# Four graph layers on one core: the start of layer 1 written as one list of 58 steps

## The chip, the cores and the metric

The kernel runs on one core of a Trainium2 chip. Its time is the device time of one execution in microseconds (us). A core has five engines that run side by side, each with its own queue of instructions that it works off in order: TensorE (PE, with PEld for the loading of weights), VectorE (DVE), ScalarE (ACT), GpSimd (POOL) and SyncE (SP, which here only issues transfers). They wait for one another through semaphores, and a waiting instruction holds up everything behind it in its own queue.

## The reference, cut to what matters

There are 2708 nodes with 128 features, and a sparse adjacency matrix of 2708 x 2708 with some 16 entries in a row. Four layers follow one another, each `x = x + layer(relu(layernorm(x)), adj)`. The change is at the seam of layers 0 and 1:

```python
# layer 0: columns of adj, weighted sum over the degree
h = jnp.maximum(_layernorm(x, axis=-1), 0.0)
msg = jnp.matmul(adj.T, h)
inv_deg = 1.0 / adj.sum(axis=0)            # 0 where it is infinite
x = x + msg * inv_deg[:, None]
# layer 1: a message for every pair of nodes, summed with the weights of adj
h = jnp.maximum(_layernorm(x, axis=-1), 0.0)
s = h @ msg_w[:, :D].T                     # source part
d = h @ msg_w[:, D:].T                     # destination part
messages = gelu(s[:, None, :] + d[None, :, :] + msg_b)
aggregated = jnp.einsum('ijd,ij->id', messages, adj)
new = jnp.concatenate([h, aggregated], axis=-1) @ upd_w.T + upd_b
g = gelu(new) + h
x = x + layernorm(g) * ln_w + ln_b
```

Layers 2 (a GRU cell) and 3 (two attention heads over the neighbours) aren't touched.

## The kernel before, in words

**Tiles.** The 2708 rows are cut into 22 tiles of 128 (`NT`), and these into six groups of four tiles, the last of two (`GROUPS`). The columns are cut into 22 blocks of 124 (`NB`, `JB`).

**Layer 0** reads `adj` tile by tile. PE multiplies it with the normed rows into six banks, and turns it around for a copy `adjT` in memory that layers 2 and 3 use. DVE scans it: for every row and every block the eight largest values (`val`) and their columns (`col`), by one `max` and one `max_index` each, 484 of each. This list of entries is what layer 1 works from. The sums of layer 0 lie turned (features down, nodes along) in `sumT`, whose memory is also `hT`, the turned input of layer 1.

**Layer 1** treats the listed entries alone. For a tile `t` it builds, step by step:

- `count_rows(t)`: how many entries each row has in each block (`rows_n`).
- `rank(t)`: a product with the triangle `before` gives, for each block, how many entries stand ahead of a row's own (`ends`, `ends4`).
- `select_rows(t)`: a compare gives the 0/1 matrix `sel` (entry slot against row), and two transfers bring a copy of it moved by one row, `later`. `finish_rows(t)` subtracts the copy, which leaves one row per slot.
- `describe(t)`: packs values (split into three bfloat16 parts), columns and `ends` into `xb`. There are two such buffers.
- `fetch(t, half)`: 11 small products of `sel` and `xb` bring each slot its row's description. `place(t)` picks from it the slot's own value and column (`value`, `where`) and builds `mine`.
- `pass_on(t)`: `where` is turned on PE, copied on ACT (`where_T`), written to memory and read back to all partitions (`spread`). `columns(t)` compares it into `cols`.
- `put_values(t)` (8 blocks on POOL) and `put_more(t, k)` (14 blocks on ACT, in five shares) make `put`, which carries a slot's value into its row.

Then the main work: `combine(t, k)` takes four blocks at a time, six products each (three for the source part with `sel` and `s3`, three for the destination part with `cols` and `d3`), `activate(t, k)` takes Gelu of them on ACT, and `gather(t, k)` sums them with `put`. `sources(k)` makes `s3` for two tiles, and the term of the diagonal. `s3` and `d3` are numbers split into three bfloat16 parts: a cast on ACT, a subtract on DVE into a scratch tile, a cast on ACT, and a subtract on POOL (the helper `split`).

**Periods.** `period(t)` lays the steps of several tiles side by side: the main work of tile `t`, `put`, `pass_on` and `columns` of `t+1`, `fetch` and `place` of `t+2`, and `rank`, `describe`, `select_rows` and `finish_rows` of `t+3`. The whole of layer 1 stands in `tc.manual_schedule()`: each engine's queue has its instructions in the order in which the program text makes them.

**The prologue** brings in what the first period needs. For each group `g` it has four steps. `enter(g)` turns the sums back on PE, adds them to `xs` on DVE (scaled by `inv_deg`), and takes the statistics of the norm, with a power on POOL (`moments`, L116 to L119). `rows_and_turn(g)` has five small DVE operations (`factors`, L125 to L129) and the norm with Relu on ACT (`scale_rows`, L135). `turn_rows(g)` turns these rows into `hT` on PE with a copy on ACT (L153, L155). `destinations(g)` multiplies them with `msg_w` into `p_d` and splits that into `d3` (L324 to L327). The groups run as a pipeline of depth four, and whole periods are put between them: `period(-3)` after the round of group 0, `period(-2)` after that of group 2, `period(-1)` after that of group 4. `sources(0)` comes at the end, then `period(0)`.

Three buffers matter in what follows: `p_m` (two banks, for `enter` and for `combine`), the tag `r` (one bank, for `p_r` of `rank`, `p_w` of `pass_on`, `p_s` of `sources` and `p_u`), and the tag `sb` (one scratch tile, for `sources` and for the split of `destinations`).

The constants of layer 1 (`count`, `count_h`, `ident_h`, `part`, `before`, the zeroed `later`, the row numbers in `xb`) lie in a pool that is opened after layer 0 and takes over its memory.

Of the kernel before, what the change touches and what calls it, by code (L numbers as in the profile page):

```python
# [20 lines left out]
F32 = mybir.dt.float32  # L21
# [9 lines left out]
P = 128  # L31
# [24 lines left out]
def width(b):  # L56
    return min(JB, N - b * JB)
# [3 lines left out]
def listed_layers(ctx: ExitStack, tc: tile.TileContext, x, adj, w, out, flag):  # L61
# [8 lines left out]
    def bank(name):  # L70
        return ps.tile([P, CH], F32, tag="ps", name=name)
# [73 lines left out]
    def span(t, k):  # L145

        return t * P, min(k * P, N - t * P)
# [18 lines left out]
    total = keep.tile([P, NT], F32, name="total")  # L166
    inv = keep.tile([P, NT], F32, name="inv_deg")

    sumT = keep.tile([D, N], F32, name="hT1")
# [102 lines left out]

    HB = NB // 2
    HP = 8
    R = 4
    C = 4 * S + R + 1  # L280
    with (
        tc.tile_pool(name="l1c", bufs=1) as fix,
        tc.tile_pool(name="l1i", bufs=2) as work,
# [18 lines left out]
        count = fix.tile([P, P], F32, name="count")  # L302
        nc.gpsimd.iota(count, [[1, P]], base=0, channel_multiplier=0, allow_small_or_imprecise_dtypes=True)
        count_h = fix.tile([P, P], BF16, name="count_h")
        nc.vector.tensor_copy(count_h, count)
        ident_h = fix.tile([P, P], BF16, name="ident_h")
        nc.vector.tensor_copy(ident_h, ident)
        part = fix.tile([P, 1], F32, name="part")
        nc.gpsimd.iota(part, [[0, 1]], base=0, channel_multiplier=1, allow_small_or_imprecise_dtypes=True)
        before = fix.tile([P, P], BF16, name="before")  # L310
        nc.vector.tensor_scalar(before, count, part, None, ALU.is_gt)
        ends4 = fix.tile([P, NB, R], BF16, name="ends4")
        rows_n = fix.tile([P, NT, NB], BF16, name="rows_n")
        ends = fix.tile([P, NT, NB], BF16, name="ends")
        later = fix.tile([P, NB, E], BF16, name="later")
        nc.gpsimd.memset(later, 0.0)
        d3 = fix.tile([P, NB, 3, D], BF16, name="d3")
        xb = [fix.tile([P, NB, C], BF16, name=f"xb{q}") for q in range(2)]
        for q in range(2):
            nc.vector.tensor_copy(xb[q][:, :, 4 * S : 4 * S + R], part.unsqueeze(1).to_broadcast([P, NB, R]))  # L320

        def split(dst, src, rest):

            nc.scalar.copy(dst[0], src)  # L324
# [268 lines left out]

        GB = (NB + 3) // 4

        def period(t):

            now, c, b, a = (0 <= t + q < NT for q in range(4))
            last = 0 <= t - 1 < NT
            if c:  # L600
                put_values(t + 1)
            for k in range(GB):
                if now:
                    combine(t, k)
# [24 lines left out]
                if k > 0 and c:  # L629
                    put_more(t + 1, k)  # L630
                if k == 3 and c:
                    columns(t + 1)
                if k == 3 and b:
                    place(t + 2)
                if k == 4 and a:
                    finish_rows(t + 3)


        def enter(g):

            t, k = GROUPS[g]
            p = mpool.tile([P, 4, D], F32, name="p_m")
            for q in range(k):
                m = size(t + q)
                nc.tensor.transpose(p[0:m, q, :], sumT[:, (t + q) * P : (t + q) * P + m], ident)
            for q in range(k):
                m = size(t + q)
                nc.vector.scalar_tensor_tensor(
                    xs[0:m, t + q, :], p[0:m, q, :], inv[0:m, t + q : t + q + 1], xs[0:m, t + q, :],
                    op0=ALU.mult, op1=ALU.add,  # L650
                )
            state["m", g] = moments(tiles_of(xs, t, k), "n1")

        def rows_and_turn(g):
            t, k = GROUPS[g]
            scale_rows(tiles_of(h, t, k), tiles_of(xs, t, k), *factors(*state.pop(("m", g))), AF.Relu)

# [5 lines left out]
        done = [0]  # L663

        def destinations(g):

            c, n = span(*GROUPS[g])
            while done[0] < NB and done[0] * JB + width(done[0]) <= c + n:
                b0 = done[0]
                bn = 1  # L670
                while bn < 4 and b0 + bn < NB and (b0 + bn) * JB + width(b0 + bn) <= c + n:
                    bn += 1
                p = bank("p_d")
                pv = p.rearrange("p (b d) -> p b d", b=4)
                for b in range(b0, b0 + bn):
                    k = width(b)
                    nc.tensor.matmul(pv[0:k, b - b0, :], hT[:, b * JB : b * JB + k], msg_wT[:, 1, :], start=True, stop=True)
                rest = once.tile([P, 4, D], F32, tag="sb", name="d_r")
                whole = bn if width(b0 + bn - 1) == JB else bn - 1
                for q0, q1, k in ((0, whole, JB), (whole, bn, width(NB - 1))):  # L680
                    if q1 > q0:
                        split(
                            [d3[0:k, b0 + q0 : b0 + q1, q, :] for q in range(3)], pv[0:k, q0:q1, :], rest[0:k, q0:q1, :]
                        )
                done[0] = b0 + bn
# [837 lines left out]
```

## Time and profile before

| | |
|---|---|
| time, median of three | 1119.21 us (1118.8 to 1120.24) |
| span of the profiled execution | 1117.6 us |
| PE busy | 966.6 us, 86% of the span |
| DVE busy | 840.2 us, 75% |
| ACT busy | 504.0 us, 45% |
| POOL busy | 393.4 us, 35% |
| end of the scan (last `max_index`, DVE) | 241.7 us |
| first product of `combine(0, 0)` | 313.66 us |
| first Gelu of `activate(0, 0)` | 317.85 us |

The upper rows are averages over stages that have different limits, and say little on one of them. The lower three, from the timeline, mark out the stage that is changed: from the end of the scan to the first Gelu. The 40 slices of the span show it as a dip of PE (a digit is the busy share in tenths):

```profile
PE   3988887932489999999999988999979999999993
DVE  5999999997647667687777364656668987997673
```

One slice is 27.9 us. DVE is at 9 up to the ninth slice (layer 0), PE falls to 3, 2 and 4 in slices 9 to 11, and stands at 9 from the twelfth on, through the periods of layer 1.

### The profile page before, as it was taken

The page shows a single profiled execution, that of the slowest core. Times are in us where ns is not written, and L with a number is a line of the kernel's source. Part 1 is how long each engine was busy: PE and PEld are TensorE (multiplying, and loading weights), DVE is VectorE, ACT ScalarE, POOL GpSimd, SP SyncE. Part 2 cuts the span into 40 slices and gives each one's busy share as a digit, 9 for nine tenths or more (in the row PEclk, how much of TensorE's full clock was granted, in tenths as well). Part 3 has the DMA queues.
Part 4 walks back from the last instruction along what each step waited for, and adds up shares of the span by engine and source line. Part 5 has one row for each costly group of instructions (what it writes and reads, how often), then busy time and mean ns, then how long its engine had stood idle before and what let it go on. Part 6 is the DMA issues. An engine that isn't in the chain of part 4 may idle for free. (4 is left out here: it accounts for less than half of the span.)

```text
span 1117.6 us, 21914 instructions
## 1 busy us (share of the span) xinstructions
PE 966.6 (86%) x7968; PEld 763.3 (68%) x7968; DVE 840.2 (75%) x2948; ACT 504.0 (45%) x1319; POOL 393.4 (35%) x466
## 2 busy tenths in 40 slices
PE   3988887932489999999999988999979999999993
PEld 1554444512379999989898953444468899999772
DVE  5999999997647667687777364656668987997673
ACT  3966656622556666666665631433322200230143
POOL 3111112102546656666665343354301200250132
PEclk9999898755589999999999988999989999999996
DMA  9497886521113332232332046555300000000000
GB/s 357 187 312 261 309 294 241 186 61 51 53 56 102 106 105 102 82 106 79 105 105 79 28 144 211 186 198 199 99 18 1 1 9 1 1 20 1 2 15 14
DMA packets 55298, 125.39 MB, mean 112 GB/s; under 512 B 7414, under 2 KB 19782, under 8 KB 52472
## 3 DMA queue, kind: packets, MB, share of 16 engines
q1 hardware_dynamic: 48590, 121.12, 31.2%
q10 hardware_dynamic: 6590, 2.77, 1.0%
q8 instruction: 64, 1.05, 0.4%
q14 instruction: 54, 0.44, 0.1%
HBM read 77.30 MB, written 30.84 MB: 97 GB/s over the span
## 5 line engine op out<-in xcount | busy, mean ns | idle before, releaser
L804 PE MATMUL att<-hv,wt 128*128 128x129 f32 (+2 forms) x1936 | 240.7, 281 | 9.2 <-DVE wt L772 9.2
L804 PEld LDWEIGHTS att<-hv,wt 128*128 128x128 f32 (+2 forms) x1936 | 221.8, 190 | 26.3 <-DVE wt L772 8.7
L772 DVE SCALAR_TENSOR_TENSOR wt<-row,lift,mask 128x1024 f32<-128x1024 f32 (+5 forms) x176 | 160.0, 939 | 34.2 <-PE att L804 34.1
L423 POOL TENSOR_SCALAR put<-mine,value 128x128 f32<-128x128 bf16 x176 | 144.8, 839 | 74.2 <-DVE mine L339 71.8
L499 PE MATMUL p_m<-s,sel 128*128 128x128 bf16 x1452 | 161.9, 220 | 7.7 <-ACT g L511 4.7
L503 PE MATMUL p_m<-d,cols 124*128 124x128 bf16 (+1 forms) x1452 | 161.7, 219 | 1.4 <-DVE cols L453 1.3
L119 POOL TENSOR_TENSOR n_r<-n_r,minus_half 128x4 f32<-128x4 f32 (+1 forms) x36 | 48.3, 1343 | 298.5 <-DVE n_r L118 289.6
L196 PE MATMUL acc<-a,hs 128*128 128x512 f32 (+2 forms) x264 | 122.3, 599 | 24.7 <-DMA a<-in_adj 17.9
L524 PE MATMUL agg<-put,g 128*128 128x128 f32 (+1 forms) x968 | 135.9, 281 | 0.0
L925 PE MATMUL p_agg<-a,hs 128*128 128x512 f32 (+2 forms) x264 | 111.1, 562 | 8.2 <-DVE u L572 4.1
L524 PEld LDWEIGHTS agg<-put,g 128*128 128x128 f32 x968 | 118.2, 192 | 0.0
L217 DVE FIND_INDEX8 col<-val,a 128x8 uint16<-128x124 f32 (+1 forms) x441 | 117.9, 278 | 0.0
L499 PEld LDWEIGHTS <-sel 128*128 128x128 bf16 x1452 | 104.1, 98 | 13.3 <-issue 9.5
L503 PEld LDWEIGHTS <-cols 124*128 124x128 bf16 (+1 forms) x1452 | 102.3, 98 | 2.5 <-DVE cols L453 1.9
L511 ACT ACTIVATE g<-p_m 128x512 f32<-128x512 f32 x132 | 73.0, 553 | 65.6 <-PE p_m L503 64.5
L216 DVE MAX8 val<-a 128x8 f32<-128x124 f32 (+1 forms) x441 | 101.8, 269 | 0.0
L431 ACT ACTIVATE put<-mine,value 128x128 f32<-128x128 bf16 x308 | 100.5, 390 | 0.0
L225 PEld LDWEIGHTS p_T<-ident,a 128*128 128x128 f32 x484 | 59.6, 147 | 56.3 <-ACT aT L229 27.0
L196 PEld LDWEIGHTS acc<-a,hs 128*128 128x128 f32 (+1 forms) x264 | 49.4, 207 | 69.0 <-issue 41.8
L225 PE MATMUL p_T<-ident,a 128*128 128x128 f32 x484 | 78.4, 295 | 20.8 <-DMA a<-in_adj 10.2
L229 ACT ACTIVATE aT<-p_T 128x512 f32<-128x512 f32 (+2 forms) x132 | 70.9, 540 | 43.6 <-issue 16.8
L925 PEld LDWEIGHTS p_agg<-a,hs 128*128 128x128 f32 (+1 forms) x264 | 48.5, 196 | 57.0 <-issue 56.0
(228 smaller groups left out, 1407.1 us busy)
## 6 DMA issues: line engine op xcount, KB each, us to landing
a<-in_adj SPq DMA_DIRECT2D x21, 1354.0 KB
adjT<-aT SPq DMA_DIRECT2D x105, 256.0 KB
a<-adjT SPq DMA_DIRECT2D x20, 1280.0 KB
spread<-passed SPq DMA_DIRECT2D x22, 704.0 KB
later<-sel SPq DMA_DIRECT2D x22, 616.0 KB
later<-sel SPq DMA_DIRECT2D x22, 82.5 KB
adjT<-aT SPq DMA_DIRECT2D x21, 74.0 KB
a<-adjT SPq DMA_DIRECT2D x4, 370.0 KB
```

The lines of the kernel that those rows point to most:

```text
L196: nc.tensor.matmul(accs[ci][:, 0:cw], h[0:m, n, :], a[0:m, c : c + cw], start=(n == 0), stop=(n == NT - 1))
L216: nc.vector.max(val[:, n, b, :], ab)
L217: nc.vector.max_index(col[:, n, b, :], val[:, n, b, :], ab)
L225: nc.tensor.transpose(p[0:k, q * P : q * P + m], a4[0:m, q, j * P : j * P + k], ident[0:m, 0:m])
L423: nc.gpsimd.tensor_scalar(st["put", 0][:, b, :], st["mine"][:, b, :], st["value"][:, b : b + 1], None, ALU.mult)
L431: nc.scalar.activation(st["put", 1][:, b - HP, :], st["mine"][:, b, :], AF.Identity, scale=st["value"][:, b : b + 1])
L499: nc.tensor.matmul(p[:, b - b0, :], st["sel"][:, b, :], s3[:, q, t % 2, :], start=(q == 0), stop=False)
L503: nc.tensor.matmul(p[:, b - b0, :], st["cols"][0:kb, b, :], d3[0:kb, b, q, :], start=False, stop=(q == 2))
L524: nc.tensor.matmul(agg, g[:, b - 4 * k, :], put, start=(b == 0), stop=False)
L772: nc.vector.scalar_tensor_tensor(wt[0:kj, :], row[0:kj, k, c : c + n], lift[0:kj, j, k : k + 1], mask[0:kj, j, c : c + n], op0=ALU.max, op ...
L804: nc.tensor.matmul(banks[s // 3][0:m, s % 3, :], wt[0:kj, q * P : q * P + m], hv[0:kj, j, k, :], start=(v < 2 and s // 3 not in touched), ...
L925: nc.tensor.matmul(pa[:, 0:n], h[0:k, j, :], a[0:k, j - j0, 0:n], start=(j == 0), stop=(j == NT - 1))
```

## The change

It does three things. The constants of layer 1 are made ahead of layer 0, in a pool that stays open through both layers. The pipeline over groups with whole periods between is replaced by one list of 58 small steps in an order written by hand, in which `enter`, `rows_and_turn` and `destinations` are each cut in two (`spread_sums` and `enter`; `rows` and `turn_rows`; `destinations` up to the first cast, and `split_destinations`). And the last two groups' destinations are put into period 0 (`fourth` ahead of `combine(0, 0)`, `fifth` ahead of `combine(0, 1)`), where the puts of tile 1 move behind them. A part of `destinations` now always takes four blocks, `4 * g` onwards, where it took as many as the turned rows allowed. The arithmetic is the same. The aim is to keep the engines from standing still one after the other between the two layers.

```diff
@@ ahead of layer 0
+    count = keep.tile([P, P], F32, name="count")
+    nc.gpsimd.iota(count, [[1, P]], base=0, ...)
+    count_h = keep.tile([P, P], BF16, name="count_h")
+    nc.vector.tensor_copy(count_h, count)
+    ident_h = keep.tile([P, P], BF16, name="ident_h")
+    nc.vector.tensor_copy(ident_h, ident)
+    part = keep.tile([P, 1], F32, name="part")
+    nc.gpsimd.iota(part, [[0, 1]], base=0, ...)
+    before = keep.tile([P, P], BF16, name="before")
+    nc.vector.tensor_scalar(before, count, part, None, ALU.is_gt)
...
+    later = keep.tile([P, NB, E], BF16, name="later")
+    nc.gpsimd.memset(later, 0.0)
+    xb = [keep.tile([P, NB, C], BF16, name=f"xb{q}") for q in range(2)]
+    for q in range(2):
+        nc.vector.tensor_copy(xb[q][:, :, 4 * S : 4 * S + R], part.unsqueeze(1).to_broadcast([P, NB, R]))
@@ after layer 0: the same lines, with fix.tile for keep.tile, are taken out
@@ def period
-        def period(t):
+        def period(t, between=()):
...
-            if c:
+            if c and not between:
                 put_values(t + 1)
             for k in range(GB):
+                for step in between[k : k + 1]:
+                    step()
                 if now:
                     combine(t, k)
@@ enter, rows, destinations
-        def enter(g):
+        def spread_sums(g):
 
             t, k = GROUPS[g]
             p = mpool.tile([P, 4, D], F32, name="p_m")
             for q in range(k):
                 m = size(t + q)
                 nc.tensor.transpose(p[0:m, q, :], sumT[:, (t + q) * P : (t + q) * P + m], ident)
+            state["p", g] = p
+
+        def enter(g):
+
+            t, k = GROUPS[g]
+            p = state.pop(("p", g))
...
-        def rows_and_turn(g):
+        def rows(g):
...
+        def blocks_of(g):
+
+            return 4 * g, min(4, NB - 4 * g)
 
         def destinations(g):
 
...
+            for src, dst, q0, q1, k in state["d", g]:
+                nc.scalar.copy(dst[0], src)
+
+        def split_destinations(g):
+
+            rest = once.tile([P, 4, D], F32, tag="sb", name="d_r")
+            for src, dst, q0, q1, k in state.pop(("d", g)):
+                r = rest[0:k, q0:q1, :]
+                nc.vector.tensor_tensor(r, src, dst[0], ALU.subtract)
+                nc.scalar.copy(dst[1], r)
+                nc.gpsimd.tensor_tensor(dst[2], r, dst[1], ALU.subtract)
@@ the order
         with tc.manual_schedule():
-            for t in range(4):
-                count_rows(t)
-            steps = (enter, rows_and_turn, turn_rows, destinations)
-            fill = {0: -3, 2: -2, 4: -1}
-            for g in range(len(GROUPS) + len(steps) - 1):
-                for k in reversed(range(len(steps))):
-                    if 0 <= g - k < len(GROUPS):
-                        steps[k](g - k)
-                if g in fill:
-                    period(fill[g])
-            sources(0)
-            for t in range(NT + 1):
+            for step, n in (
+                (spread_sums, 0), (count_rows, 0), (spread_sums, 1), (rank, 0), (enter, 0),
+                (select_rows, 0), (describe, 0), (enter, 1), (spread_sums, 2), (rows, 0), (turn_rows, 0),
+                (count_rows, 1), (rows, 1), (count_rows, 2), (count_rows, 3), (destinations, 0), (turn_rows, 1),
+                (finish_rows, 0), (fetch_both, 0), (rank, 1), (enter, 2), (spread_sums, 3), (select_rows, 1),
+                (split_destinations, 0), (destinations, 1), (describe, 1), (rows, 2), (turn_rows, 2),
+                (place, 0), (pass_on, 0), (sources, 0), (enter, 3), (spread_sums, 4), (split_destinations, 1),
+                (destinations, 2), (rows, 3), (turn_rows, 3), (finish_rows, 1), (fetch_both, 1), (enter, 4),
+                (spread_sums, 5), (columns, 0), (place, 1), (split_destinations, 2), (destinations, 3), (rows, 4),
+                (turn_rows, 4), (enter, 5), (rank, 2), (select_rows, 2), (rows, 5), (turn_rows, 5), (describe, 2),
+                (split_destinations, 3), (put_values, 0), (destinations, 4), (put_rest, 0), (finish_rows, 2),
+            ):
+                step(n)
+
+            def fourth():
+                split_destinations(4)
+                destinations(5)
+
+            def fifth():
+                split_destinations(5)
+                put_values(1)
+
+            period(0, (fourth, fifth))
+            for t in range(1, NT + 1):
                 period(t)
```

More of the change, by code (lines that the diff above doesn't have):

```diff
@@ L167, in listed_layers @@
     inv = keep.tile([P, NT], F32, name="inv_deg")
+    HB = NB // 2
+    HP = 8
+    R = 4
+    C = 4 * S + R + 1
+    count = keep.tile([P, P], F32, name="count")
+    nc.gpsimd.iota(count, [[1, P]], base=0, channel_multiplier=0, allow_small_or_imprecise_dtypes=True)
+    count_h = keep.tile([P, P], BF16, name="count_h")
[3 more added lines that the diff above has]
+    part = keep.tile([P, 1], F32, name="part")
+    nc.gpsimd.iota(part, [[0, 1]], base=0, channel_multiplier=1, allow_small_or_imprecise_dtypes=True)
+    before = keep.tile([P, P], BF16, name="before")
+    nc.vector.tensor_scalar(before, count, part, None, ALU.is_gt)
+    ends4 = keep.tile([P, NB, R], BF16, name="ends4")
+    rows_n = keep.tile([P, NT, NB], BF16, name="rows_n")
+    ends = keep.tile([P, NT, NB], BF16, name="ends")
+    later = keep.tile([P, NB, E], BF16, name="later")
[3 more added lines that the diff above has]
+        nc.vector.tensor_copy(xb[q][:, :, 4 * S : 4 * S + R], part.unsqueeze(1).to_broadcast([P, NB, R]))
     sumT = keep.tile([D, N], F32, name="hT1")
@@ L270, in layer3_weights @@
             nc.vector.tensor_copy(src_w[:, k, :], w_x[:, 2 * D + 2 + k : 2 * D + 3 + k].to_broadcast([P, P]))
[L277 to L280, printed above, removed]
     with (
@@ L299, in listed_layers @@
         nc.vector.tensor_tensor(src_self[:, 1, :], msg_wT[:, 0, :], msg_wT[:, 1, :], ALU.add)
[L302 to L316, printed above, removed]
         d3 = fix.tile([P, NB, 3, D], BF16, name="d3")
-        xb = [fix.tile([P, NB, C], BF16, name=f"xb{q}") for q in range(2)]
-        for q in range(2):
-            nc.vector.tensor_copy(xb[q][:, :, 4 * S : 4 * S + R], part.unsqueeze(1).to_broadcast([P, NB, R]))
         def split(dst, src, rest):
@@ L661, in turn_rows @@
             turn(hT[:, c : c + n], bank("p_h1"), lambda q: h[:, t + q, :], k, t, nc.scalar.copy)
-        done = [0]
+        def blocks_of(g):
+            return 4 * g, min(4, NB - 4 * g)
         def destinations(g):
[L667 to L685, printed above, removed]
@@ L687, in listed_layers @@
-        with tc.manual_schedule():
-            for t in range(4):
-                count_rows(t)
-            steps = (enter, rows_and_turn, turn_rows, destinations)
-            fill = {0: -3, 2: -2, 4: -1}
-            for g in range(len(GROUPS) + len(steps) - 1):
-                for k in reversed(range(len(steps))):
-                    if 0 <= g - k < len(GROUPS):
-                        steps[k](g - k)
-                if g in fill:
-                    period(fill[g])
-            sources(0)
-            for t in range(NT + 1):
+            b0, bn = blocks_of(g)
@@ new lines, in destinations @@
+            p = bank("p_d")
+            pv = p.rearrange("p (b d) -> p b d", b=4)
+            for b in range(b0, b0 + bn):
+                k = width(b)
+                nc.tensor.matmul(pv[0:k, b - b0, :], hT[:, b * JB : b * JB + k], msg_wT[:, 1, :], start=True, stop=True)
+            whole = bn if width(b0 + bn - 1) == JB else bn - 1
+            state["d", g] = [
+                (pv[0:k, q0:q1, :], [d3[0:k, b0 + q0 : b0 + q1, q, :] for q in range(3)], q0, q1, k)
+                for q0, q1, k in ((0, whole, JB), (whole, bn, width(NB - 1)))
+                if q1 > q0
+            ]
@@ new lines, in destinations, with fetch_both @@
+            for src, dst, q0, q1, k in state["d", g]:
[7 more added lines that the diff above has]
+                nc.gpsimd.tensor_tensor(dst[2], r, dst[1], ALU.subtract)
+        def fetch_both(t):
+            for half in range(2):
+                fetch(t, half)
@@ new lines, in put_rest @@
+        def put_rest(t):
+            for k in range(1, GB):
+                put_more(t, k)
+        with tc.manual_schedule():
+            for step, n in (
[19 more added lines that the diff above has]
+            for t in range(1, NT + 1):
```

## The prediction

> **What bounds the kernel now.** I read the busy shares by slice first: the scan of layer 0 ends near 241 us, TensorE (PE) is almost without a gap from about 320 to 645 us (the periods of layer 1), and between them lies a stretch in which no engine is full and PE does little. The table by stage puts numbers on it. Columns: length, busy time (instructions) of PE, PEld, DVE, ACT, POOL, granted clock, DMA share, GB/s.
>
> ```profile
> 200.00:250.00 50.00, 31.12 (x113) 18.80 (x111) 49.72 (x315) 21.66 (x81) 5.58 (x11) 0.59 0.34 114
> 241.50:313.70 72.20, 24.38 (x137) 19.85 (x138) 51.75 (x167) 25.44 (x68) 27.43 (x33) 0.52 0.15 48
> 331.00:345.00 14.00, 14.00 (x207) 13.74 (x205) 12.56 (x18) 8.91 (x27) 12.13 (x12) 1.00 0.33 105
> 450.00:550.00 100.00, 94.30 (x1315) 90.68 (x1313) 74.75 (x144) 63.47 (x184) 65.60 (x80) 1.00 0.29 95
> ```
>
> Until 241.5 DVE is full (max and max-index of the scan). From 241.5 to 313.7, the prologue, DVE works 51.75 of 72.2 us and is still the busiest; its 20 us of idling and its 52 us of work are what can be shortened. After that PE is the bound, so a period that starts 1 us sooner ends 1 us sooner. The timeline, in order of time, shows where the idling is (start, length, engine, line, ..., idle time before it and what ended it):
>
> ```profile
> 241.62 0.13 DVE L252 TENSOR_TENSOR gate_b<-b_ih,b_hh 128x2 f32<-128x2 f32 x1
> 243.46 0.25 POOL L303 IOTA count<- 128x128 f32 x1 [21.13 <-DVE inv_deg L243]
> 243.74 2.52 DVE L305 CAST count_h<-count 128x128 bf16<-128x128 f32 x1
> 243.88 2.44 DVE L311 TENSOR_SCALAR before<-count,part 128x128 bf16<-128x128 f32 x1
> 246.47 0.18 PE L348 MATMUL p_r<-rows_n,before 128*128 128x22 bf16 x1 [12.79 <-DVE before L311]
> ...
> 258.23 1.62 DVE L370 TENSOR_TENSOR sel<-sel,later 128x2816 bf16<-128x2816 bf16 x1 [4.86 <-DMA later<-sel]
> ...
> 260.76 1.65 ACT L135 ACTIVATE hs<-xs,n_r 128x128 f32<-128x128 f32 x4 [8.52 <-DVE n_r L129]
> ...
> 277.35 0.62 ACT L326 CAST d<-d_r 124x512 bf16<-124x512 f32 x1 [7.41 <-DVE d_r L325]
> ...
> 302.63 0.69 DVE L325 TENSOR_TENSOR d_r<-p_d,d 124x512 f32<-124x512 f32 x1 [1.60 <-ACT d L324]
> 307.31 0.69 DVE L325 TENSOR_TENSOR d_r<-p_d,d 124x512 f32<-124x512 f32 x1 [3.13 <-ACT d L324]
> 310.50 0.29 DVE L325 TENSOR_TENSOR d_r<-p_d,d 124x128 f32<-124x128 f32 x1 [2.50 <-ACT d L324]
> 312.48 0.69 DVE L474 TENSOR_TENSOR sb<-p_s,msg_b 128x512 f32<-128x512 f32 x1 [0.87 <-POOL d L327]
> 313.66 0.26 PE L499 MATMUL p_m<-s,sel 128*128 128x128 bf16 x1 [1.86 <-ACT s L324]
> 317.85 0.60 ACT L511 ACTIVATE g<-p_m 128x512 f32<-128x512 f32 x1 [0.89 <-PE p_m L503]
> ```
>
> Three things are to be seen. Constants are made in the middle of the path, and two small DVE operations take 2.5 us beside a POOL memset. DVE stands 4.86 us on the first shifted copy `later`, with the norm of group 0 queued behind it. From 302 on DVE mostly waits: groups 4 and 5 and `sources(0)` run one behind the other (PE, ACT, DVE, ACT, POOL), and only then does the first `combine` start, at 313.66.
>
> **What the skill says.** The Trainium skill, "SBUF — State Buffer", section "SBUF: two separate sides", says that DVE and GpSimd share one port pair as an exclusive lock: who starts first holds it for the whole instruction. The trace agrees: L305 took 2.52 us beside the 2.44 us memset of `later`, where the same cast of `ident_h` (L307) took 0.23; and eight puts on POOL took 5.86 us at 288.28, with DVE compares beside them, but 4.67 at 315.23. "DMA: Bandwidth & Descriptors", section "Anatomy of one DMA", gives some 2.0 us fixed cost for a transfer; here `later` took 4.86 us from the compare to the subtract, so I use that. "ScalarE: Activation LUTs", section "What ACT_TABLE_LOAD costs", gives 1283 ns for a load; the trace has 1.28 at 314.52, before the first Gelu.
>
> **The change part by part, on the path.** I lay the new order out engine by engine with the durations of before. DVE steps with no wait between them start about 0.08 us before the last has ended (the four adds at 248.42, 0.34 each, take 1.12).
>
> *Constants made early.* The iotas and the memset fall on POOL where it is idle (it does nothing until 12.99 us): nothing. The five DVE operations stand in DVE's queue behind the norm statistics, just before `offdiag` (18.58 us in the trace), and from there DVE is the bound of layer 0. At about 0.15 us each they cost 0.7: the scan ends at 242.2. What they cost in the prologue goes: from 243.3 to 246.4 about 3 us.
>
> *Head.* From there to `inv_deg` took 1.67 us (241.62 to 243.29); `rank(0)` now stands between: a reduce, a round trip to PE (0.6) and two casts, so 2.8: 245.0. Then `enter(0)`: four adds at 0.26, four pairs of statistics at 0.39, two small ones: 2.9. But `src_self` now stands among them and waits for `msg_wT`, whose load is issued just after `inv_deg`. Before, the load was issued at 243.40 and `src_self` at 248.09 did not wait, so it takes at most 4.7 us and, by the skill's fixed cost, at least 2; I take 3. DVE idles 1.0, and everything queued behind, `select_rows(0)` too, starts at 249.1 (bounds: 248.1 to 250.8).
>
> *Group 0 beside the first tile's copy.* The compare (1.53), then `v_r` (0.26) and `enter(1)` (2.9) to 253.7 run while `later` is under way (250.7 + 4.9 = 255.6); the factors of group 0 (1.0) and of group 1, and three counts, too. So the 4.86 us wait is filled. `rows(0)` starts on ACT at 254.8, where it was 260.76: 6 us won here. The subtract ends at 258.6. The next wait is new: `rank(1)` stands on PE behind `destinations(0)`, `turn_rows(1)` and 22 `fetch` products, so DVE idles 2.2 to 260.8.
>
> *Middle.* `enter(2)` 2.9, compare 1.5, `d_r` 0.6, a wait of 1.6 for ACT's cast ahead of `v_r`, factors 1.0: 268.9. `place(0)` 4.3 (270.43 to 274.86 before), then `sources(0)` with two waits of 0.65: 275.2. `enter(3)`, `d_r`, a wait of 0.6 for POOL's power, factors, subtract: 282.1. `enter(4)` 2.9, `cols` 0.9 (its transfers have landed by then; before it waited 2.35), `place(1)` 4.3, `d_r` and factors: 291.3. `enter(5)` 1.5, a wait of 1.3 for `rank(2)`, casts, compare 1.5, factors of group 5: 297.1.
>
> *Tail.* `rows(5)` on ACT, transposes, copy of `hT`: 299.1. `destinations(4)` and `(5)` on PE: the first `combine` at 301.1, where it was 313.66. `sources(0)` with its table load is off the tail. The splits of groups 4 and 5 are in period 0, where `combine(0, 4)` comes some 8 us later: hidden there, but ACT, in its order, first does 14 puts at 0.30 (4.2 us) and the casts of 4 and 5. So the first Gelu comes at 306.5 and PE, which has two banks `p_m`, stands about 3.4 us at `rank(3)` for ACT's copy of `where_T`. From 317.85 to 306.5 is 11.3.
>
> *Correction.* The order of before, laid out in the same way, gives its first Gelu at 316.5, 1.4 us before the trace, and the first one after the fourth `combine` at 325.8 for 327.44. The sums are thus short by what ports and issue add. Against 325.8 the new order gives 315.6: a gain of 10.2, which a PE-bound rest keeps. 1119.2 - 10.2 = 1109.0 us.
>
> **The rivals.**
> 1. *New waits give half back*: 1114. POOL's power (1.01) now often starts just behind a compare and by the lock is held until it ends, 2.5; I have put it on the path once, for 0.6. For it: four groups by 1.5 is 6. Against: before two of the groups the factors are queued behind a whole `enter`, which covers it. The ACT queue at the entry could stretch likewise.
> 2. *More is won*: 1104. If `msg_wT` lands in time (1.0), the scan isn't delayed (0.7), and POOL, PE and ACT are ready at the waits of 2.2, 1.6 and 1.3 us. Against: these waits follow from the order of the queues.
> 3. *No gain*: 1118.5. The prologue gets shorter but period 0 and 1 wait for what was put into them (`put_values(1)` now behind six splits on POOL, 14 puts on ACT), so that the PE-bound stretch is entered no sooner. For it: ACT holds the first Gelu 5.4 us after the first `combine` (4.2 before). Against: the puts of tile 1 are first needed by its own `gather`, over 15 us later; 8 by 0.58 to 0.84 us is under 7.
> 4. *Slower*: 1122. The waits of DVE in the fixed order, 12 us by my count, come out twice as long, and the constants bring a port wait of 2.5 us into the scan: 12 + 2.5 - 11.3 = +3. Against: at the constants' place the memset is long over.
>
> **How the numbers follow.** Forecast, within 3 us of 1109: 0.70. Rival 1: 0.14; rival 2: 0.08; rival 3: 0.05; rival 4: 0.03. For 8 times in 10 the range takes the forecast with the bounds of the load (1.0 less to 1.7 more), of the correction (0 to 3) and most of rivals 1 and 2: 1105 to 1114. Faster by over 0.2% (2.2 us) are the forecast and rivals 1 and 2, and a part of rival 3: 0.93; within: 0.04; slower: 0.03.
>
> **What would show it right or wrong.** In the profile of the changed kernel: the last max-index ends 0.5 to 1 us later than 241.69; `rows(0)` on ACT near 255; the subtract of tile 0 with next to no wait for DMA; DVE waits for `p_r` of 2 us near 260 and of 1 near 294; first `combine` near 302 and first Gelu near 307 to 308; PE then waits once, for `where_T`; later periods some 14 us apart as before. I am wrong if the first Gelu comes after 313, if the scan ends over 2 us later, or if the distance from first Gelu to the end is longer than the 799.8 us (1117.6 - 317.85) of before.

## The result, and the profile after

The changed kernel took 1110.17 us (median of four runs, 1109.5 to 1111.89) where the kernel before took 1119.01 us (four runs, 1118.21 to 1120.24): a ratio of 0.9922, 95% interval 0.9905 to 0.9940. Forecast were 1109.0 us and a range of 1105 to 1114. The gain is 8.8 us for 10.2.

The busy shares by slice of the changed kernel (tenths; a slice is now 27.7 us):

```profile
PE   3998887944389999999999979999979999999993
DVE  5999999997766668676887255655578977997673
```

PE's dip now reads 4, 4, 3 in slices 9 to 11, where it read 3, 2, 4: PE is a little fuller there, and DVE has 7, 7, 6 for 7, 6, 4 in slices 10 to 12. (The twelfth slice of PE is an 8 in both.) The table by stage (length, busy time and instructions of PE, PEld, DVE, ACT, POOL, granted clock, DMA share, GB/s), with the first line from the end of the scan to the first `combine`, to be held against the second line of the prediction's table:

```profile
244.30:304.10 59.80, 23.79 (x133) 18.20 (x133) 47.18 (x158) 22.92 (x54) 16.71 (x20) 0.59 0.17 57
321.90:335.80 13.90, 13.90 (x207) 13.64 (x205) 12.50 (x18) 9.02 (x27) 10.45 (x12) 1.00 0.30 106
450.00:550.00 100.00, 94.80 (x1324) 91.35 (x1323) 76.51 (x158) 64.50 (x189) 64.59 (x80) 1.00 0.26 89
```

The prologue is 59.8 us long where it was 72.2: DVE's idling in it fell from 20.5 to 12.6 us, its work from 51.75 to 47.18. A period and the stretch from 450 to 550 are as before. The timeline of the changed kernel, with the lines that answer to those of before and the new waits (start, length, engine, line, operation, idle time before it and what ended it):

```profile
244.04 0.26 DVE L241 FIND_INDEX8 col<-val,near 128x8 uint16<-128x104 f32 x1
...
249.02 0.23 DVE L318 COPY src_self<-msg_wT 128x128 f32<-128x128 f32 x1
250.05 1.62 DVE L339 TENSOR_TENSOR sel<-count_h,ends 128x2816 bf16<-128x2816 bf16 x1
250.22 2.31 POOL L119 TENSOR_TENSOR n_r<-n_r,minus_half 128x4 f32<-128x4 f32 x1 [25.29 <-DVE n_r L118]
255.68 1.65 ACT L135 ACTIVATE hs<-xs,n_r 128x128 f32<-128x128 f32 x4 [3.36 <-DVE n_r L129]
258.02 1.61 DVE L370 TENSOR_TENSOR sel<-sel,later 128x2816 bf16<-128x2816 bf16 x1
262.24 0.18 DVE L349 CAST ends<-p_r 128x22 bf16<-128x22 f32 x1 [2.60 <-PE p_r L348]
...
303.93 4.20 ACT L431 ACTIVATE put<-mine,value 128x128 f32<-128x128 bf16 x14
304.06 0.53 PE L499 MATMUL p_m<-s,sel 128*128 128x128 bf16 x3
304.53 6.04 POOL L423 TENSOR_SCALAR put<-mine,value 128x128 f32<-128x128 bf16 x8
308.86 0.59 ACT L511 ACTIVATE g<-p_m 128x512 f32<-128x512 f32 x1
309.63 0.17 PE L348 MATMUL p_r<-rows_n,before 128*128 128x22 bf16 x1 [2.14 <-ACT where_T L441]
311.72 0.49 DVE L697 TENSOR_TENSOR d_r<-p_d,d 124x128 f32<-124x128 f32 x2 [5.10 <-POOL d L699]
312.45 0.59 ACT L511 ACTIVATE g<-p_m 128x512 f32<-128x512 f32 x1
```

The reader is to see four things. DVE no longer stands 4.86 us at the subtract L370: the copy `later` has landed by 258.02. The norm of group 0 starts on ACT at 255.68, 5.1 us sooner. First `combine` and first Gelu come 9.6 and 9.0 us sooner. But the scan ends at 244.30, 2.6 us later than the 241.69 of before. From the end of the scan to the first Gelu the new order takes 64.6 us for 76.2, so 11.6 us are won and 2.6 are given back. In the first period a wait of 5.10 us is left on DVE, behind POOL's eight puts.

### The profile page after: what moved, and what is told of

The parts are those of the page before. It is cut to its first block, busy times and chain, and to the rows that moved or that the text cites. A ratio compares the mean times of both kernels' runs of the same rounds, so it can differ in the third digit from the quotient of the medians.

```text
span 1108.1 us, 21904 instructions
## 1 busy us (share of the span) xinstructions
PE 963.6 (87%) x7968; PEld 760.1 (69%) x7968; DVE 839.4 (76%) x2948; ACT 504.2 (46%) x1319; POOL 394.1 (36%) x466
## 5 line engine op out<-in xcount | busy, mean ns | idle before, releaser
L423 POOL TENSOR_SCALAR put<-mine,value 128x128 f32<-128x128 bf16 x176 | 147.7, 855 | 72.4 <-DVE mine L339 70.0
L119 POOL TENSOR_TENSOR n_r<-n_r,minus_half 128x4 f32<-128x4 f32 (+1 forms) x36 | 51.3, 1425 | 316.1 <-DVE n_r L118 305.2
L220 PEld LDWEIGHTS acc<-a,hs 128*128 128x128 f32 (+1 forms) x264 | 49.7, 209 | 72.2 <-issue 43.4
```

What stands on the lines that cost most here:

```text
L220: nc.tensor.matmul(accs[ci][:, 0:cw], h[0:m, n, :], a[0:m, c : c + cw], start=(n == 0), stop=(n == NT - 1))
L423: nc.gpsimd.tensor_scalar(st["put", 0][:, b, :], st["mine"][:, b, :], st["value"][:, b : b + 1], None, ALU.mult)
```

## The experiments

All marks in the table are read from the timelines; the thirteenth Gelu is the first of tile 2 and stands for the PE-bound stretch that follows. Each time is a median, and each ratio is against runs of the kernel before beside it on the same chip (medians 1118.95 for the first four rows below the line of the changed kernel, 1118.34 for those marked with one star, 1119.68 for two), so that ratios, not times, are compared across groups. An interval is some 1 to 2 us to each side; parts below that are read off the marks, which come from one profiled execution of each kernel.

| kernel | scan ends | first combine | first Gelu | 13th Gelu | time, us | ratio (95%) |
|---|---|---|---|---|---|---|
| before | 241.69 | 313.66 | 317.85 | 345.13 | 1119.01 | |
| changed | 244.30 | 304.06 | 308.86 | 336.12 | 1110.17 | 0.9922 (0.9905 to 0.9940) |
| constants alone | 244.31 | 312.96 | 317.15 | 345.54 | 1119.55 | 1.0004 (0.9996 to 1.0013) |
| list alone | 241.40 | 303.81 | 308.61 | 335.90 | 1108.72 | 0.9912 (0.9898 to 0.9925) |
| constants ahead of the norms | 241.62 | 301.83 | 306.63 | 333.89 | 1107.15 | 0.9893 (0.9878 to 0.9908) |
| no fold | 244.64 | 304.84 | 313.27 | 342.29 | 1115.04 | 0.9964 (0.9950 to 0.9978) |
| memset ahead of the norms * | 241.16 | 301.25 | 306.05 | 333.33 | 1107.02 | 0.9896 (0.9881 to 0.9912) |
| ACT's puts in period 0 * | 244.18 | 304.35 | 307.80 | 340.68 | 1113.56 | 0.9955 (0.9942 to 0.9969) |
| own scratch * | 243.97 | 303.95 | 308.75 | 335.09 | 1106.76 | 0.9894 (0.9879 to 0.9910) |
| first, scratch and puts * | 241.42 | 300.99 | 304.42 | 333.15 | 1104.61 | 0.9874 (0.9859 to 0.9889) |
| no fold, own scratch ** | 244.27 | 304.35 | 310.06 | 338.42 | 1109.68 | 0.9908 (0.9892 to 0.9923) |
| first and scratch ** | 241.47 | 301.21 | 306.01 | 332.35 | 1105.8 | 0.9873 (0.9858 to 0.9889) |
| sources last ** | 244.18 | 307.08 | 311.97 | 339.69 | 1113.51 | 0.9943 (0.9929 to 0.9957) |

### Where the scan's 2.6 us come from

The start of layer 0 in the changed kernel's timeline:

```profile
12.72 3.23 POOL L119 TENSOR_TENSOR n_r<-n_r,minus_half 128x4 f32<-128x4 f32 x3 [11.26 <-DVE n_r L118]
15.99 2.44 POOL L188 MEMSET later<- 128x2816 bf16 x1
16.12 0.29 DVE L125 TENSOR_TENSOR n_r<-n_r 128x4 f32<-128x4 f32 x3
16.33 0.30 DVE L126 TENSOR_TENSOR n_r<-n_r 128x4 f32<-128x4 f32 x3
16.55 2.07 DVE L127 TENSOR_SCALAR n_r<-n_r 128x4 f32<-128x4 f32 x3
18.53 0.39 POOL L229 COPY near<-a 128x248 f32<-128x248 f32 x1
18.64 0.72 DVE L128 TENSOR_TENSOR n_r<-n_r 128x4 f32<-128x4 f32 x3
19.28 0.50 DVE L129 SCALAR_TENSOR_TENSOR n_r<-n_mv,n_r 128x4 f32<-128x4 f32 x3
```

Two of these operations in the kernel before:

```profile
16.38 0.61 DVE L125 TENSOR_TENSOR n_r<-n_r 128x4 f32<-128x4 f32 x3
...
17.14 0.30 DVE L127 TENSOR_SCALAR n_r<-n_r 128x4 f32<-128x4 f32 x3
```

The memset doesn't run early, although POOL stands idle for 11.26 us up to 12.72: the text puts it behind the norm loop, so in POOL's queue it stands behind three powers that wait for DVE's statistics. It runs at 15.99, and DVE's L127, 0.30 us for three in the kernel before, is held until it has ended. From DVE's first statistics to the end of the scan it takes 233.3 us where it took 230.4. Counting for each operation what it adds beyond the end of the one ahead, of the 2.9 more 2.1 lie in the factors of the norm (L125 to L129), 0.7 in the five operations of the constants and 0.1 in idle time.

**Constants alone**: the kernel before with nothing but the constants moved.

```diff
@@ ahead of layer 0
+    count = keep.tile([P, P], F32, name="count")
...
+    later = keep.tile([P, NB, E], BF16, name="later")
+    nc.gpsimd.memset(later, 0.0)
@@ behind src_self in layer 1
-        count = fix.tile([P, P], F32, name="count")
...
-        later = fix.tile([P, NB, E], BF16, name="later")
-        nc.gpsimd.memset(later, 0.0)
```

> The kernel before with the constants made early, in the same lines as in the changed kernel, and the old pipeline over groups. Theory (3 us out of the head of the prologue, 2.5 us into the scan): scan ends near 244, 1118.5 us, within 1 us of the kernel before. Rival (the constants bring the greater part of the gain): 1114 to 1116 us.

Measured: 1119.55 us over 13 runs, ratio 1.0004 (0.9996 to 1.0013). The scan ends at 244.31, as in the changed kernel. The first Gelu comes 0.7 us sooner than before, the thirteenth 0.4 later. The constants as placed bring nothing.

**List alone**: the same lines moved the other way in the changed kernel.

```diff
@@ ahead of layer 0
-    count = keep.tile([P, P], F32, name="count")
...
-    nc.gpsimd.memset(later, 0.0)
@@ behind src_self in layer 1
+        count = fix.tile([P, P], F32, name="count")
...
+        nc.gpsimd.memset(later, 0.0)
```

> The list of 58 steps alone; the constants are made after layer 0 again, in the pool of layer 1. Theory (the order of the steps brings the gain; making the constants early gives about as much back in the scan as it takes out of the prologue): the scan ends at 241.7 us as in the kernel before, since the 2.5 us by which it ended later in the changed kernel go; the head of the prologue is some 3 us longer again; first Gelu near 309; about 1110.7 us, within 1 us of the changed kernel. Rival (the constants are the larger part of the gain): 1113 us or more.

Measured: 1108.72 us, 10.2 below the kernel before beside it. In its timeline the two small operations are held again, in the prologue:

```profile
243.44 2.52 DVE L304 CAST count_h<-count 128x128 bf16<-128x128 f32 x1
243.44 2.45 POOL L315 MEMSET later<- 128x2816 bf16 x1
243.59 2.44 DVE L310 TENSOR_SCALAR before<-count,part 128x128 bf16<-128x128 f32 x1
```

From the end of the scan to the first Gelu it takes 67.2 us, 2.65 more than the changed kernel, and its scan ends 2.9 sooner. So the early constants do take nearly 3 us out of the prologue, and put the same into layer 0.

**Constants ahead of the norms**: the pool and the constants made before the norm loop of layer 0 (the list's tiles, `val`, `col` and three small ones, are then declared behind it).

```diff
-    for t, k in GROUPS:
-        normalise(h, xs, t, k, AF.Relu, "n0")
     late = ctx.enter_context(tc.tile_pool(name="late", bufs=1))
...
     for q in range(2):
         nc.vector.tensor_copy(xb[q][:, :, 4 * S : 4 * S + R], part.unsqueeze(1).to_broadcast([P, NB, R]))
+    for t, k in GROUPS:
+        normalise(h, xs, t, k, AF.Relu, "n0")
```

> The changed kernel with the same constants made ahead of the norm of layer 0, where DVE and POOL wait for the first load of x until about 11 us. Theory (the scan ended 2.5 us later because the memset of later stood in POOL's queue behind the powers of the norm, at 16.0 us, and held DVE's L127 for 2.07 us by the shared port, and because five small DVE operations, 0.75 us in all, stood ahead of the scan): L127 takes 0.3 us again, the scan ends at 241.5 to 242, and the time falls by 2.3 to 2.6 us against the changed kernel, to about 1107.7. Rival (the later end is one of arrival of the loads, or of the scan itself): the scan still ends near 244 and the time stays at 1110.

Measured: 1107.15 us. Its timeline has the memset where POOL is free, and L127 back at its old length:

```profile
1.50 2.44 POOL L179 MEMSET later<- 128x2816 bf16 x1
...
19.80 0.30 DVE L127 TENSOR_SCALAR n_r<-n_r 128x4 f32<-128x4 f32 x3
```

The scan ends 2.7 us sooner than in the changed kernel, as the theory said, and every later mark comes 2.2 us sooner. By the ratios the time falls by about 3 us, for 2.3 to 2.6 forecast, which is within the intervals.

**Memset ahead of the norms**: `later` alone moved up, with the pools that it needs, to tell the memset from the five DVE operations.

```diff
+    later = keep.tile([P, NB, E], BF16, name="later")
+    nc.gpsimd.memset(later, 0.0)
     for t, k in GROUPS:
         normalise(h, xs, t, k, AF.Relu, "n0")
...
-    later = keep.tile([P, NB, E], BF16, name="later")
-    nc.gpsimd.memset(later, 0.0)
```

> The changed kernel with only the pool and the memset of later (POOL, 2.44 us) moved ahead of the norms of layer 0; the iotas and the five DVE operations of the constants stay where the change put them. Tells the two parts of the 2.6 us apart by which the scan ends later. Theory (1.8 us are the memset's hold on DVE's L127 at 16.55 and what stands behind, 0.8 us are the five operations themselves): the scan ends at 242.4 to 242.7 and the time is 1107.8 to 1108.6. Rival 1 (the five operations, and their wait for POOL's iotas, are the larger part): the scan ends past 243.5 and the time is above 1109.3. Rival 2 (the five operations are hidden once the memset is away): the scan ends at 241.6, 1107.2, as in a2.

Measured: scan end 241.16, 1107.02 us. The scan's end and the time are those of rival 2, which called the five operations hidden, but the trace doesn't show them hidden: they still take 0.7 us of DVE. What makes up for it is that the factors of the norm take 0.8 us less than in the kernel before. With the memset away the scheduler orders layer 0's start another way: six of the scan's `max` operations stand ahead of L125, and L125 to L129 then run with no operation of POOL beside them, 0.29 to 0.30 us for three each, where L125 had 0.61 in the kernel before, which is a part of the 0.8. So moving the memset alone takes the whole loss away. My split of 1.8 and 0.8 is near what the changed kernel's trace shows (2.1 and 0.7), but as a forecast it was wrong, as it did not reckon with the new order.

### Whether the order of the list matters

**Sources last**: `sources(0)` back to near the end of the list.

```diff
-                (place, 0), (pass_on, 0), (sources, 0), (enter, 3), (spread_sums, 4), (split_destinations, 1),
+                (place, 0), (pass_on, 0), (enter, 3), (spread_sums, 4), (split_destinations, 1),
...
-                (turn_rows, 4), (enter, 5), (rank, 2), (select_rows, 2), (rows, 5), (turn_rows, 5), (describe, 2),
+                (turn_rows, 4), (enter, 5), (rank, 2), (select_rows, 2), (rows, 5), (turn_rows, 5), (sources, 0), (describe, 2),
```

> The changed kernel with sources(0) moved from behind pass_on(0) to behind turn_rows(5), where the kernel before had it, near the end of the list. Theory (its chain of PE, DVE, ACT, DVE, ACT and POOL and ACT's table load, about 5 us one behind the other, then stands in front of the first combine, and DVE gets only its 2.6 us in the middle back): first combine 1 to 3 us later than 304.06, time 1111.2 to 1113.2. Rival (it lies beside the split of group 4, the puts and destinations at the tail as well, so its place doesn't matter): 1109 to 1110.6.

Measured: 1113.51 us, ratio 0.9943. The timeline of the tail:

```profile
300.31 0.69 DVE L474 TENSOR_TENSOR sb<-p_s,msg_b 128x512 f32<-128x512 f32 x1 [3.38 <-PE p_s L467]
302.35 1.28 ACT L483 ACT_TABLE_LOAD   x1
306.07 1.22 PE L682 MATMUL p_d<-msg_wT,hT 128*124 128x128 f32 x4 [4.15 <-DVE d_r L697]
307.08 0.53 PE L499 MATMUL p_m<-s,sel 128*128 128x128 bf16 x3
```

The first `combine` comes 3.0 us later than in the changed kernel, at the upper end of what the theory said: DVE waits 3.38 for the sources' products, ACT loads its table in front of the cast that DVE's `v_r` waits for, and PE's products for group 5 wait 4.15 for the `d_r` behind it. All marks after it are later by 3.1 to 3.6, and the time is 0.3 us above the theory's window. This one step's place is worth 3.0 to 3.6 us by the marks, about 2.4 by the ratios.

### What the fold into period 0 is worth, and what limits the first period

**No fold**: the splits of groups 4 and 5 and the destinations of group 5 ahead of period 0 (the puts of tile 1 then stand at the head of the period, on POOL still behind these splits).

```diff
+            split_destinations(4)
+            destinations(5)
+            split_destinations(5)
-            period(0, (fourth, fifth))
-            for t in range(1, NT + 1):
+            for t in range(NT + 1):
                 period(t)
```

> The changed kernel with the splits of the last two groups, and the destinations of the last, ahead of period 0 instead of in it. Theory (the fold only moves the last split on ACT from ahead of the first Gelu to behind it, since PE's own order is the same): first Gelu near 312.5 instead of 308.9, second near 313 instead of 312.5, and the time 0 to 1.5 us longer than that of the changed kernel, so up to 1111.7. Rival (the fold is what took the serial tail away, 302 to 313 us in the kernel before): 4 us or more longer, 1114 or above.

Measured: 1115.04 us, ratio 0.9964 for the 0.9922 of the changed kernel, so 4.7 us worse, where I had allowed 1.5; the rival, 4 us or more, has the number. Its timeline:

```profile
312.54 0.49 DVE L697 TENSOR_TENSOR d_r<-p_d,d 124x128 f32<-124x128 f32 x2 [5.12 <-POOL d L699]
313.27 0.59 ACT L511 ACTIVATE g<-p_m 128x512 f32<-128x512 f32 x1
314.05 0.18 PE L348 MATMUL p_r<-rows_n,before 128*128 128x22 bf16 x1 [5.38 <-ACT where_T L441]
315.01 0.53 PE L499 MATMUL p_m<-s,sel 128*128 128x128 bf16 x3
320.75 0.69 DVE L474 TENSOR_TENSOR sb<-p_s,msg_b 128x512 f32<-128x512 f32 x1 [5.29 <-PE p_s L467]
```

The wait of DVE for the one scratch tile `sb`, behind POOL's eight puts, is the 5.1 us of the changed kernel. But here ACT's cast of that result stands in front of the first Gelu, and behind that in front of `where_T`, for which PE waits 5.38 us. What I had not seen: PE can't work ahead of it, having only the two `p_m` banks, and everything that stands behind `p_r` in its queue, the sources of the next tiles too, is late. A second thing comes in: after this wait PE's granted clock is low. Three products of `combine(0, 2)` take 0.53 us at 315.01, where they take 0.33 in the changed kernel (at 310.27); the granted clock is 0.54 from 314.0 to 320.4 here and 1.00 from 309.6 to 313.5 there. From `p_r` to the first product of `combine(0, 3)` PE needs 6.4 us for the work for which it needs 3.8 in the changed kernel.

**Own scratch**: two tiles of their own for the split, in place of the tag `sb`.

```diff
-            rest = once.tile([P, 4, D], F32, tag="sb", name="d_r")
+            rest = work.tile([P, 4, D], F32, name="d_r")
```

> The changed kernel with scratch tiles of their own (two buffers) for the split of destinations in place of the one tile under the tag sb. Removes DVE's wait of 5.10 us at 311.72 for POOL's subtract of group 4, behind its eight puts. Theory (that wait hardly matters in the changed kernel, since PE has products to do until the second Gelu): the second Gelu moves from 312.45 to 310.5 to 311.5, PE's wait for the third part shrinks, the time falls by 0 to 1 us: 1109.2 to 1110.2. Rival (the scratch tile is what ties the first period to POOL): 2 us or more, below 1108.2.

Measured: 1106.76 us, ratio 0.9894. The timeline has DVE's wait at 2.41, and the second Gelu 2.7 us sooner:

```profile
308.94 0.49 DVE L697 TENSOR_TENSOR d_r<-p_d,d 124x128 f32<-124x128 f32 x2 [2.41 <-POOL put L423]
309.52 0.17 PE L348 MATMUL p_r<-rows_n,before 128*128 128x22 bf16 x1 [2.28 <-ACT where_T L441]
309.78 0.58 ACT L511 ACTIVATE g<-p_m 128x512 f32<-128x512 f32 x1
```

The time speaks for the rival, the marks for the theory: the thirteenth Gelu comes 1.0 us sooner, not 3, and 0.3 of that is an earlier end of the scan. The rest appears only between layers 1 and 2 (about 1.4 us, between 634 and 713 us) and further on. From the thirteenth Gelu to the end of the span the profiles show 769.8 us here, 769.6 and 770.0 in two of the other versions with these tiles ("first, scratch and puts" and "no fold, own scratch"), but 771.6 in the third ("first and scratch"); the nine kernels without them have 770.7 to 772.5. Up to 615 us, while PE is the bound, this one, the changed kernel and the kernel before run alike to within 0.2 us. So whether the tiles shorten the rest stays open; what moves that seam by up to 2 us was not tried.

**No fold, own scratch**: both of these edits.

```diff
-            rest = once.tile([P, 4, D], F32, tag="sb", name="d_r")
+            rest = work.tile([P, 4, D], F32, name="d_r")
...
+            split_destinations(4)
+            destinations(5)
+            split_destinations(5)
-            period(0, (fourth, fifth))
```

> The splits of groups 4 and 5 and the destinations of group 5 ahead of period 0 again (as in a3, 1115.04), but with scratch tiles of their own (as in a5, 1106.76). Theory (what the fold saved was the wait for the one scratch tile behind POOL's eight puts, which in a3 stood in front of the first Gelu and so of where_T and PE): without that wait the first Gelu comes at 309.5 to 310.5 where a3 had 313.27, and the time is 0.5 to 2 us above a5: 1107.2 to 1108.8. Rival (the fold is worth its 4.9 us whatever the scratch, since ACT has to do the casts of group 5 ahead of the first Gelu anyway): 1111 to 1112.

Measured: first Gelu 310.06, as the theory said; 1109.68 us, ratio 0.9908, above the theory's window and under the rival's. By the thirteenth Gelu it is 3.3 us behind "own scratch" (338.42 and 335.09), where "no fold" is 6.2 behind the changed kernel; by the ratios it is 1.6 and 4.7. So about half of what the fold wins, or more, is that it takes the wait for the scratch tile off the first Gelu. Of the 3.3 us that stay by the marks, 1.6 are the granted clock again: from `p_r` to `combine(0, 3)` PE takes 5.4 us here and 3.8 in "own scratch", and the clock is 0.66 from 311 to 316. Why it is low is not shown, and the length of the wait alone doesn't decide it: PE waits 1.82 us for `where_T` here, and 2.14 in the changed kernel, which keeps the full clock.

**ACT's puts in period 0**: tile 0's 14 puts spread over the period, as for later tiles.

```diff
-                (split_destinations, 3), (put_values, 0), (destinations, 4), (put_rest, 0), (finish_rows, 2),
+                (split_destinations, 3), (put_values, 0), (destinations, 4), (finish_rows, 2),
...
-            period(0, (fourth, fifth))
+            def sixth():
+                put_more(0, 1)
+                put_more(0, 2)
+
+            period(0, (fourth, fifth, sixth, *(lambda k=k: put_more(0, k) for k in range(3, GB))))
```

> The changed kernel with ACT's 14 puts of tile 0 (4.2 us in the trace of after, 303.93 to 308.13) taken out of the list and spread over period 0, as in every later period. Theory (ACT's puts hold the first Gelu, which starts 4.8 us after the first combine): the first Gelu comes 3 to 4 us sooner, at about 305.5, but POOL's eight puts (6.04 us) still keep the scratch tile from DVE's subtract of group 5 until 311.7, so the second Gelu moves by less, and the time falls by 0.5 to 2 us below that of the changed kernel: 1108.2 to 1109.7. Rival 1 (the first Gelu alone sets the later order): the whole 3 to 4 us, 1106 to 1107. Rival 2 (ACT only moves its 4.2 us into period 0, where they stand in front of the Gelus that PE waits for): no gain, 1109.5 to 1111.

Measured: 1113.56 us, 2.6 us above the highest that any of the three said. The timeline:

```profile
306.96 0.62 ACT L698 CAST d<-d_r 124x512 bf16<-124x512 f32 x1 [2.62 <-DVE d_r L697]
307.80 0.61 ACT L511 ACTIVATE g<-p_m 128x512 f32<-128x512 f32 x1
314.55 2.15 ACT L431 ACTIVATE put<-mine,value 128x128 f32<-128x128 bf16 x7
319.62 1.85 ACT L431 ACTIVATE put<-mine,value 128x128 f32<-128x128 bf16 x6
321.37 0.58 ACT L511 ACTIVATE g<-p_m 128x512 f32<-128x512 f32 x1
322.00 0.33 PE L499 MATMUL p_m<-s,sel 128*128 128x128 bf16 x3 [2.31 <-ACT g L511]
```

Without the puts ACT stands 2.62 us for DVE's `d_r`, which is behind the subtract L370, so the first Gelu comes only 1.1 us sooner. And each gap between later Gelus now has the puts of two tiles, six or seven where it had two or three: the fourth Gelu comes at 321.37, 2.9 us later, and PE stands for it. Most of the 4.2 us of puts lay in idle time of ACT: without them the first Gelu gains only 1.1.

**First, scratch and puts**, and **first and scratch**: constants ahead of the norms and the own scratch tiles, with and without this last edit.

> Constants made ahead of the norms of layer 0 (as in a2, 1107.15), ACT's puts in period 0, and own scratch tiles for the splits, together. Theory: the scan ends at 241.6, the first Gelu comes at about 303, PE's 6.9 us of waits between 304 and 320 shrink to 3 or 4, and the time is 1104.5 to 1106. Rival (the two edits of the tail only push one another's waits around; PE still stands for POOL's puts): the time is that of a2, 1106.5 to 1107.5.

> Constants ahead of the norms of layer 0 (a2, 1107.15) and scratch tiles of their own for the splits (a5), with ACT's puts left in the list. Theory (the two gains lie in different stages and add, and moving the puts gave a6 next to nothing): 1103.6 to 1104.8. Rival (a6's 1104.61 needed the puts moved into period 0): 1105.2 to 1107.

Measured: ratios 0.9874 (0.9859 to 0.9889) and 0.9873 (0.9858 to 0.9889), 1104.61 and 1105.8 us on two chips. The first is in its theory's window, though its first Gelu comes at 304.42 for 303. By the ratios, and within their intervals, the gains of the constants' place and of the scratch add, as the theory of the second said; the absolute 1105.8 is in the rival's window, on the chip on which the kernel before took 1119.68. Moving the puts is not needed: with it the first Gelu comes 1.6 us sooner, and the thirteenth 0.8 later. That is far less than the 4.6 us by which the puts alone delay the thirteenth, so most of that loss does not come where the tiles are their own; how the two work together was not followed. Either version beats both kernels.

## Why the prediction was right, and where it was off

The mechanism is the one forecast; one term of the sum was mis-sized, and a sign that the prediction had set for being wrong came: the scan ends 2.61 us later, where over 2 was to count. The two others did not come: the first Gelu is at 308.86, not after 313, and from there to the end it takes 799.2 us for 799.8. By its own steps:

- **Constants made early**: this step failed. "Nothing" on POOL and 0.7 on DVE, scan end at 242.2, became 2.6 us and 244.30. The prediction took POOL's idle time until 13 us for the place of the memset, and so against rival 4 "at the constants' place the memset is long over". POOL was idle because the head of its queue was waiting, and the memset stands behind that head. The port wait of 2.5 us that rival 4 named did come into layer 0 (L127 to L129 took 2.4 us longer), and with the memset moved up it was gone (scan ends of 241.16 and 241.62). The 0.7 for the five operations was right. The other half of the step holds: 2.65 us left the prologue.
- **Head**: forecast a wait of 1.0 for `msg_wT`; there was none. The load was issued at 246.92 and `src_self` ran at 249.02 without waiting, so it took at most 2.1. The section "Anatomy of one DMA" of the Trainium skill, "DMA: Bandwidth & Descriptors", on which the lower bound of 2 rests, describes transfers that GpSimd issues, and this one is issued by ACT; the trace, with an upper bound alone, neither bears the 2 out nor speaks against it. The compare came 5.8 us after the end of the scan, for 6.9.
- **Group 0 beside the first tile's copy**: as forecast, by the timeline; no run takes this step out alone. The 4.86 us wait is gone, `rows(0)` came 11.4 us after the end of the scan (12.6 forecast), the new wait for `p_r` took 2.60 (2.2).
- **Middle and tail**: first `combine` 59.8 us after the end of the scan (58.9), first Gelu 64.6 (64.3), PE's stand at `rank(3)` 2.14 (3.4). That the early `sources(0)` takes a piece off the tail was shown by putting it back, 3.0 us at the first `combine`. That the splits are "hidden" in period 0 is right of the first Gelu, but the step didn't name DVE's wait of 5.10 behind POOL's puts, worth some 0.7 to 1.4 us by the marks of the two versions without it ("own scratch" against the changed kernel, "first and scratch" against "constants ahead of the norms", each less the shift of its scan's end).
- **Correction and sum**: to the fourth Gelu the new order took 74.1 us from the end of the scan, where the layout had 73.4; the old took 85.8, where it had 84.1. So the prologue won 11.6 for 10.7, the scan lost 2.6 for 0.5, and the sum at the fourth Gelu is 9.0 for 10.2. The PE-bound rest kept it, as forecast (9.0 at the thirteenth Gelu). That the sum came so near is in part luck: the prologue won 0.9 more than laid out, which hides a part of the 2.1 by which the scan was mis-sized. With that loss taken away ("constants ahead of the norms") the change wins 11.8 us, 1.6 more than forecast. Of the 10.2 that the list alone wins, the place of `sources(0)` and the fold were tried one by one; the rest is read from the timeline. In the working itself a few sums are loose: `place(0)` took 4.43 before and not 4.3, and the steps from 282.1 to `enter(5)` add up to 291.8 and not 291.3.
- **Rivals**: none came true as a whole. New waits did arise, as rival 1 said (the power held to 2.31 us behind a compare at 250.22 and to 2.32 at 265.49, DVE's 5.10), but from the end of the scan to the fourth Gelu the whole still gained 0.9 us more than laid out.

What the memset costs where it does run fits the Trainium skill: "SBUF — State Buffer", section "Who interferes with whom", says that a DVE operation with two inputs in SBUF contends only with a GpSimd operation that reads SBUF, and a `tensor_scalar` in a two-port mode with any. The trace agrees row by row: beside the memset, which reads nothing, the `TENSOR_TENSOR` rows L125 and L126 took 0.29 and 0.30 us, and the `TENSOR_SCALAR` L127 took 2.07; L128 and L129, with two inputs, took 0.72 and 0.50 beside POOL's copies L229, which read. That L127 runs in a two-port mode no trace shows. And where in POOL's queue the memset stands is read from the program alone: this is what the prediction missed.

## What to carry to other kernels

An engine that is idle in the profile is not free: look at what stands at the head of its queue, and put work meant for the idle time ahead of that, not merely early in the text. When a chain is moved off the critical path into a later stage, look in that stage for the one buffer and the in-order queue through which it still holds others up; here one scratch tile behind eight puts was about half of what the move was worth at the thirteenth Gelu. And work that lies in idle time, like ACT's 14 puts, can get dearer when it is spread over a stage in which that engine feeds the bound: here by 4.6 us with the one scratch tile, by 0.8 with tiles of their own.

## What of the hardware was not expected

That a memset on POOL lets two rows of DVE operations on 128x4 tiles pass and holds the third, of the same shape but another kind (0.29, 0.30 and 2.07 us), was not in my reading of the profile of before, where the two operations beside the memset, a cast and a `TENSOR_SCALAR`, were both held (2.52 and 2.44 us). A 128 KB load of weights was there at most 2.1 us after its issue (246.92 to 249.02), where I had taken 3. And the granted clock of PE fell after waits of 5.38 and 1.82 us (to 0.54 and 0.66), but not after one of 2.14; why, no run here shows.
